# Block 2's projections as seven products of halves, with the weight sums made in place during block 0's FFN

## The chip, the cores and the metric

The kernel runs on one core of one Trainium2 chip. The metric is the device time of one launch in microseconds (us); smaller is better. A time comes from runs without a profile; the profile comes from one more execution, whose own time is given beside its span.

## What is computed

`x` is 4 sequences of 1024 tokens with 512 features in float32, 4096 tokens in all. The reference, cut to what matters:

```python
xn  = layernorm(x)
q, v, g = xn @ Wq.T, xn @ Wv.T, silu(xn @ Wg.T)        # three 512 x 512 projections
ret = scan(lam * state + v)                            # along the tokens of a sequence
out = (layernorm(q * ret) * gamma + beta) * g
x1  = x + layernorm(out @ Wo.T)
h   = layernorm(x1)
up, gate = (h @ fp8(up_w)) * us, silu((h @ fp8(gate_w)) * gs)      # 512 -> 1536
y   = x1 + layernorm(((gate * up) @ fp8(down_w)) * ds)             # 1536 -> 512
```

The FFN weights are rounded to fp8 values first, and the kernel also looks for weights that are too large for fp8 (the "search"), whose finding it adds to the output's scale.

## The kernel before

**Blocks and their overlap.** The tokens are cut into `NB` = 8 blocks of 512. A block has an attention part (class `Retention`) and an FFN part (class `Ffn`). The main loop (`for t in range(NB)`, line 973) does three things at once: the FFN of block t (`f`), the attention of block t+1 (`b`), and the loading, normalizing and transposing of block t+2 (`n`); `l` is the FFN of block t-1, of which the last layernorm and the store are left. Each turn of `t` has twelve steps `i`, one for each 128 of the 1536 hidden features. I write "turn t" and "step i" for these.

**Order.** Every engine's instructions run in the order in which the program writes them (`InOrder`, lines 66 to 74), so the order within a step is the schedule of all five engines. All profile lines therefore name line 74, and one tells instructions apart by their tiles. SyncE issues nearly all transfers (DMAs), in program order too; a transfer that must wait for data holds back those behind it.

**A step.** TensorE does the gate product (tile `pfg`), some attention work, the up product (`pfu`), and the down product (`pd`) of step i-2. Between them ScalarE does the silu of the gate, VectorE multiplies up and gate (`f.fuse`, line 1082: tile `gate<-pfu`), and ScalarE rounds that for the down product (`fuse<-gate`). `pfg` and `pfu` take turns in two PSUM banks (`ps_f`), so the up product of step i+1 can't begin before VectorE's multiplication of step i has read its bank.

**Two ways to project.** A block with `t < FAST` = 3 projects with the stored weights `wv_sb`, `wq_sb`, `wg_sb`: twelve groups of 128 output features, eight matmul instructions of 512 tokens each (functions `v`, `q`, `g_of`). A block with `t >= FAST` splits each weight matrix and its input into halves both ways and forms seven products of halves in place of eight (`product`, line 461; `order` lists them). Seven times three products need sums of input halves (`input_sums`, on GpSimd, tile `t_sums`) and sums of weight halves (`weight_sums`, tiles `sum_v` and so on). The weight sums are made once by VectorE in turn 1, steps 0 and 1, and kept in DRAM; from there they stream through `w_ring`, four slots of 256 KB, one fetch for each product, issued when a slot is free. `t_sums`, `w_ring` and `mids` lie in the places of `wv_sb`, `wq_sb` and `wg_sb`, and the first four fetches are issued at the end of turn 1, step 6.

**The end of an attention part.** In steps 7 to 10 the output projection of 128 tokens each is made (`b.o`, line 1067, tile `po`), and with it runs a chain across four engines for each group s of 128 tokens:

- `o_moments(s)` (step s+7): VectorE takes the statistics of `po`, GpSimd turns the variance into 1/std with two small instructions (`rstd_in_place`, line 262).
- `x1_of(s)` (same step, behind `f.fuse`): ScalarE normalizes `po` in blocks 0 and 1 (`shift_scale`, three instructions; VectorE does it in later blocks), GpSimd adds it to `x`, SyncE keeps the sum in DRAM (`kept`).
- `x1_moments(s)` (head of step s+8): VectorE takes the statistics of that sum, GpSimd makes 1/std.
- `x1n_of(s)`, `move_x1n(s)` (step s+8, ahead of `o_moments(s+1)` and `f.fuse`): ScalarE normalizes the sum, VectorE transposes it by 32 x 32 blocks, SyncE sends it through DRAM (`mxs`) to finish the transposition. The last group (s = 3) is transposed by TensorE instead (`turn_x1n(3)`, tile `pt`, step 11).

VectorE's statistics of `x`, its transposition, its statistics of the next `po` and its `f.fuse` stand in one queue in this order.

**The search.** 24 ScalarE instructions (tile `seen`) in turn 1, dealt out over the steps by the list `look`; `pass_over` brings their finding to `ds_sb` in turn 2, step 1.

Of the kernel before, what the change touches and what calls it, by code (L numbers as in the profile page):

```python
# [10 lines left out]
F32 = mybir.dt.float32  # L11
I32 = mybir.dt.int32
F32R = mybir.dt.float32r
F8 = mybir.dt.float8e4
AF = mybir.ActivationFunctionType
ALU = mybir.AluOpType

P = 128
# [5 lines left out]
def retention_ffn_sandwich(  # L24
# [20 lines left out]
    NT, D = x.shape  # L45
# [182 lines left out]
    def find_over():  # L228


        k = 0
        for j in range(4):
            for w in (gate_sb, up_sb, down_sb):
                v = w[:, ts(j, NI // 4), :] if w is down_sb else w[:, :, ts(j, I // 4)]
                for sign in (1.0, -1.0):
                    tag = "ret" if k >= 6 else "xn"
                    seen = work.tile(list(v.shape), F8, tag=tag, name=f"seen_{k}", bufs=2 if k >= 6 else 1)
                    act.activation(
                        seen, v.bitcast(F32), AF.Relu, bias=neg_max, scale=sign,
                        accum_out=over[:, k : k + 1], saturate=False,  # L240
                    )
                    k += 1
                    yield
# [3 lines left out]
    def pass_over():  # L247

        dve.reduce_sum(total, over, mybir.AxisListType.X)
        po = ps_tile("over_all")  # L250
        pe.matmul(po[:, :1], mean_w, total, start=True, stop=True)
        dve.tensor_scalar(total, po[:, :1], 3e38, 3e38, ALU.mult, ALU.mult)
        dve.tensor_scalar(total, total, 0.0, None, ALU.mult)
        dve.tensor_scalar(ds_sb, ds_sb, total, None, ALU.add)

# [74 lines left out]
    FAST = 3  # L330
    H = TB // 2
# [4 lines left out]
    squares = {"v": (wvT, wv_sb), "q": (wqT, wq_sb), "g": (wgT, lambda: wg_sb)}  # L336
    operands = {}

    def weight_sums():

        for k, (src, w) in squares.items():
            w = w() if callable(w) else w
            v = src.rearrange("(c p) f -> p c f", p=P)
            a11, a12, a21, a22 = (w[:, i : i + 2, o : o + H] for o in (0, H) for i in (0, 2))
            operands[k] = {1: v[:, 0:2, 0:H], 2: v[:, 2:4, 0:H], 4: v[:, 2:4, H:D]}
            done = {}
            for j, x, y, op in (
                (5, a21, a22, ALU.add), (6, 5, a11, ALU.subtract),
                (7, a11, a21, ALU.subtract), (3, a12, 6, ALU.subtract),
            ):  # L350
                t = work.tile([P, D], F32, tag="tok", name=f"sum_{k}{j}", bufs=4)
                done[j] = t.rearrange("p (c f) -> p c f", c=2)
                x, y = (done[o] if isinstance(o, int) else o for o in (x, y))
                dve.tensor_tensor(done[j], x, y, op)
                operands[k][j] = dram.tile([P, 2, H], F32, tag=f"sum_{k}{j}", name=f"dsum_{k}{j}", bufs=1)
                sp.dma_start(operands[k][j], done[j])
                yield

    sums = weight_sums()
# [481 lines left out]
    wg_sb = load_square(wgT, "wg_sb")  # L841
    a = Retention(0, x_first)
# [128 lines left out]
    look = [2, 2, 2, 0, 1, 3, 3, 3, 2, 2, 2, 2]  # L971
    l = None
    for t in range(NB):
        f, n = Ffn(a), None
        fast = b is not None and b.fast
        for i in range(NI):
# [5 lines left out]

            if l and i == 0:
                l.fetch()
# [6 lines left out]
            if l and b and not fast and i == 3:  # L991
                l.norm(0)
                l.add(0)
                l.norm(1)
                l.add(1)
# [8 lines left out]
            if n and i == 6 and t > 0:  # L1004
                n.stats(2)
                n.stats(3)
                n.rstd()
                if n.fast:
                    n.shift()
# [11 lines left out]
            if fast and i in (0, 1, 2, 3, 4, 5, 6):  # L1021
                b.product()
            if fast and i == 2:
                l.stats(0)
# [9 lines left out]
            if b and not fast and t > 0 and i < 3:  # L1034
                b.v(i + 1)
                b.scan(i + 1)
            if l and b and not fast and i == 2:
                l.stats(0)
                l.stats(1)
            if b and not fast and i == 3:  # L1040
                b.halves()
                units()
                if t == 0:
                    rounds(3, now=False)
                b.g_of(0)
                b.mean()
                b.center_y()
                if t == 0:
                    n.stats(3)
                    n.rstd()  # L1050
                    n.shift()
            if b and not fast and i == 4:
                b.halves()
                if t == 0:
                    rounds(3, now=False)
                b.g_of(1)
                b.var()
# [3 lines left out]
            if b and not fast and i == 6:  # L1061
                b.g_of(3)
                b.z(2)
                if t == 0:
                    b.z(3)
# [12 lines left out]
            if n and n.fast and i == 11:  # L1078
                n.input_sums(1, 2)
# [3 lines left out]
            if b and not fast and i == 4:  # L1083
                b.rstd_y()
            if n and i == 11:
                if n.fast:
                    n.products(2)
                else:
                    n.v(0)
                    n.scan(0)  # L1090
                b.turn_x1n(3, "pf")
                b.upper_of(3)
            if fast and i < 6:
                b.product()
# [27 lines left out]
            if l and b and not fast and i == 2:  # L1122
                l.stats(2)
                l.stats(3)
                l.rstd()
# [5 lines left out]
            if l and b and not fast and i == 3:  # L1131
                l.norm(2)
                l.add(2)
                l.norm(3)
                l.add(3)
            if b and not fast and t > 0 and i < 3:
                b.q(i + 1)
                b.y_of(i + 1)
            if b and not fast and i == 6 and t > 0:
                b.z(3)  # L1140
            if n and i == 5 and t == 1:
                n.stats(0)
                n.stats(1)
# [6 lines left out]
            if n and t > 0 and 6 <= i <= 9:  # L1150
                n.norm_x(i - 6, n.fast)
                n.send_x(i - 6)
# [7 lines left out]
            if n and i == 11:  # L1160
                if n.fast:
                    n.product()
                    n.input_sums(3, 4)
                else:
                    n.q(0)
                    n.y_of(0)
# [24 lines left out]
            if n and n.fast and i == 11:  # L1191
                n.product()
            if n and t > 1 and i == 5:
                n.stats(0)
                n.stats(1)
            if t == 1 and i < 2:
                for _ in range(6):
                    next(sums, None)
            if t == 1 and i == 6:
# [7 lines left out]
            if t == 2 and i == 1:  # L1207
                pass_over()
# [73 lines left out]
```

## Time and profile before

| | |
|---|---|
| median of 3 runs | 992.09 us (991.88 to 992.85) |
| the profiled execution, its own time | 991.89 us |
| its span, first to last instruction | 990.1 us |
| TensorE busy | 968.6 us, 98% |
| VectorE, ScalarE, GpSimd busy | 66%, 37%, 26% |
| granted TensorE clock, mean | 0.998 |
| turn 0, from its first gate product to that of turn 1 | 106.05 us |
| turn 1 | 124.78 us |
| turn 2 | 119.99 us |
| turns 3, 4, 5 | 118.59, 118.61, 118.60 us |
| turn 6 | 112.30 us |

In a line of the timeline the first number is the start in us from the start of the span, the second the time in us (of all xN instructions together); then come the engine, the operation, the tile written and the tiles read, and in brackets how long the engine sat idle before it and for whom. The list of busy time by stretches gives start:end, length, and the busy time and number of instructions of each engine.

### The profile page before, as it was taken

What the parts mean: (1) busy time and instruction counts of PE and PEld (TensorE: products, weight loads), DVE (VectorE), ACT (ScalarE), POOL (GpSimd) and SP (SyncE); (2) the same over time, 40 slices, a digit from 0 to 9 for tenths busy, and PEclk for the clock granted to TensorE, in tenths of its full rate; (3) what the DMA queues carried; (4) which work ended last, traced back from release to release, by engine and by line L of the source; (5) the groups of instructions that cost most, each with busy time, mean ns of one, the idle gap of its engine ahead of it and who ended that gap; (6) DMA issues with size and microseconds to landing.
All of it is one profiled execution on the core that took longest, in us unless ns stands there. A gap on an engine that the chain in (4) does not pass through costs nothing.

```text
span 990.1 us, 11037 instructions
## 1 busy us (share of the span) xinstructions
PE 968.6 (98%) x3878; PEld 722.0 (73%) x3878; DVE 657.1 (66%) x1006; ACT 365.3 (37%) x549; POOL 256.4 (26%) x337
## 2 busy tenths in 40 slices
PE   9999999999999999999999999999999999999996
PEld 7455766666666878678876788767887788877885
DVE  5996978548746567665686566866567656756445
ACT  3556575433765125221432114321152211512223
POOL 1405121203314033240513305132141312322020
PEclk9999999999999999999999999999999999999999
DMA  9312314412136326253243633245241542213021
GB/s 295 119 64 73 119 64 104 130 64 85 65 98 149 126 69 229 80 144 118 85 128 90 160 91 109 94 129 157 76 149 57 136 138 75 75 32 117 0 86 43
DMA packets 85223, 104.56 MB, mean 106 GB/s; under 512 B 7728, under 2 KB 49712, under 8 KB 85168
## 3 DMA queue, kind: packets, MB, share of 16 engines
q1 hardware_dynamic: 83584, 102.92, 34.5%
q10 hardware_dynamic: 1584, 0.94, 0.5%
q8 instruction: 31, 0.51, 0.2%
q14 instruction: 24, 0.20, 0.1%
HBM read 71.06 MB, written 32.77 MB: 105 GB/s over the span
## 4 chain that ended last, share of the span: by engine, by line
PE 86%; DVE 6%; POOL 3%; ACT 2%; issue 1%; DMA 1%; ACTq 0%; DVEq 0%; SPq 0%; POOLq 0%
PE pfu L74 16%; PE pfg L74 16%; PE pd L74 15%; PE pv L74 10%; PE pg L74 10%; PE pq L74 9%; PE po L74 9%; POOL t_sums L74 1%; DVE st L74 1%; DVE fuse L74 1%; POOL mv L74 1%; DVE scr L74 1%; ACT seen L74 1%; POOL x L74 1%; DVE d L74 1%
## 5 line engine op out<-in xcount | busy, mean ns | idle before, releaser
L74 PE MATMUL pfu<-x1nT,up_sb 128*128 128x512 f32 x768 | 212.1, 418 | 0.0
L74 PE MATMUL pfg<-x1nT,gate_sb 128*128 128x512 f32 x768 | 194.3, 395 | 0.4 <-DVE x1nT L74 0.4
L74 PE MATMUL pd<-down_sb,fuse 128*128 128x512 f32 x720 | 187.2, 401 | 0.0
L74 PEld LDWEIGHTS pfu<-x1nT,up_sb 128*128 128x128 f32 x768 | 144.5, 188 | 44.4 <-issue 14.4
L74 PEld LDWEIGHTS pfg<-x1nT,gate_sb 128*128 128x128 f32 x768 | 144.1, 188 | 30.4 <-DVE x1nT L74 0.8
L74 PEld LDWEIGHTS pd<-down_sb,fuse 128*128 128x128 f32 x720 | 135.3, 188 | 29.3 <-issue 1.7
L74 ACT CAST fuse<-gate 128x512 fp32r<-128x512 f32 x90 | 55.7, 618 | 236.4 <-DVE gate L74 236.4
L74 ACT ACTIVATE gate<-pfg,gs_sb 128x512 f32<-128x512 f32 x96 | 65.7, 684 | 206.2 <-PE pfg L74 206.1
L74 DVE SCALAR_TENSOR_TENSOR gate<-pfu,us_sb,gate 128x512 f32<-128x512 f32 x96 | 71.6, 746 | 82.8 <-PE pfu L74 82.8
L74 PE MATMUL po<-wo_sb,y 128*128 128x512 f32 x256 | 114.5, 592 | 0.0
L74 POOL TENSOR_SCALAR mv<-mv 128x1 f32<-128x1 f32 (+1 forms) x82 | 18.6, 226 | 302.6 <-DVE mv L74 301.6
L74 PEld LDWEIGHTS po<-wo_sb,y 128*128 128x128 f32 x256 | 48.2, 189 | 50.3 <-issue 46.9
L74 DVE TENSOR_TENSOR fuse<-gate,fuse 128x512 fp32r<-128x512 f32 x90 | 75.6, 840 | 9.1 <-ACT fuse L74 9.1
L74 POOL TENSOR_TENSOR ysum<-y 128x256 f32<-128x256 f32 (+1 forms) x13 | 13.5, 1038 | 188.8 <-DVE y L74 161.1
L74 POOL TENSOR_TENSOR x<-x,x1n 128x512 f32<-128x512 f32 x32 | 46.7, 1460 | 45.7 <-DVE x1n L74 36.7
L74 DVE BATCH_NORM_STATS2 st<-x 128x6 f32<-128x512 f32 x64 | 43.6, 681 | 13.7 <-POOL x L74 11.2
L74 DVE TENSOR_TENSOR mids<-pv,mids 128x512 f32<-128x512 f32 x25 | 17.3, 691 | 46.3 <-PE pv L74 43.4
L74 POOL TENSOR_TENSOR mv<-mv,nhalf 128x1 f32<-128x1 f32 (+1 forms) x75 | 45.3, 604 | 6.2
L74 PE MATMUL pv<-xnT,wv_sb 128*128 128x512 f32 (+1 forms) x120 | 42.9, 508 | 1.6 <-ACT xnT L74 1.6
L74 PE MATMUL pv<-t_sums,w_ring 128*128 128x256 f32 x160 | 38.3, 382 | 5.6 <-POOL t_sums L74 5.6
L74 PE MATMUL pq<-xnT,wq_sb 128*128 128x512 f32 (+1 forms) x112 | 43.4, 531 | 0.0
L74 PE MATMUL pg<-xnT,wg_sb 128*128 128x512 f32 x96 | 43.0, 592 | 0.0
(156 smaller groups left out, 1334.5 us busy)
## 6 DMA issues: line engine op xcount, KB each, us to landing
kept<-x SPq DMA_DIRECT2D x32, 256.0 KB, 2.1
x<-kept SPq DMA_DIRECT2D x32, 256.0 KB, 3.7
x<-in_x SPq DMA_DIRECT2D x28, 256.0 KB, 4.1
out<-d SPq DMA_DIRECT2D x27, 256.0 KB, 2.0
xnT<-mx SPq DMA_DIRECT2D x24, 256.0 KB, 4.8
mxs<-xs SPq DMA_DIRECT2D x84, 64.0 KB, 1.8
x1n<-mxs SPq DMA_DIRECT2D x21, 256.0 KB, 2.7
mx<-xn SPq DMA_DIRECT2D x20, 256.0 KB, 2.3
```

The source lines that it names most:

```text
L74: return lambda *args, **kwargs: tc.keep_in_program_order(op(*args, **kwargs))
```

## The change

- `FAST` is 2: block 2 uses the seven products too. It begins them in turn 0, step 11, and goes on in turn 1, which gets the order of steps that turns 2 to 6 have. The weight sums are needed one turn earlier.
- `weight_sums` runs on GpSimd, four instructions for each of q, v and g, in place of the weights, at the end of steps 7, 8 and 9 of turn 0. `keep_sums` sends each set to DRAM one step later. The first four fetches into `w_ring` are issued at the end of turn 0, step 10.
- In step 11 all four `input_sums` stand together; of v's products, one comes ahead of the transposition `turn_x1n(3)`, one behind it and one at the end of the step (before: two, one and one). The fourth moves to step 1 of the next turn.
- The search is dealt out as 5, 5, 4, 2, 0, 0, 0, 2, 2, 2, 2, 0 over turn 1's steps, and its scratch tiles change their tags.
- `pass_over` becomes a generator whose three parts stand in turn 2, step 0, between products.
- Branches that only a slow block in turn 1 used are gone (among them VectorE's scans and normalizations there).

The diff, cut to its core:

```diff
     def pass_over():
         dve.reduce_sum(total, over, mybir.AxisListType.X)
-        po = ps_tile("over_all")
+        yield
+        po = ps_tile("over_all", "pa0")
         pe.matmul(po[:, :1], mean_w, total, start=True, stop=True)
+        yield
         dve.tensor_scalar(total, po[:, :1], 3e38, 3e38, ALU.mult, ALU.mult)
...
-    FAST = 3
+    FAST = 2
...
-    def weight_sums():
-        for k, (src, w) in squares.items():
...
-                dve.tensor_tensor(done[j], x, y, op)
-                operands[k][j] = dram.tile([P, 2, H], F32, tag=f"sum_{k}{j}", name=f"dsum_{k}{j}", bufs=1)
-                sp.dma_start(operands[k][j], done[j])
-                yield
+    def weight_sums(k):
...
+        pool.tensor_tensor(a22, a21, a22, ALU.add)
+        pool.tensor_tensor(a21, a11, a21, ALU.subtract)
+        pool.tensor_tensor(a11, a22, a11, ALU.subtract)
+        pool.tensor_tensor(a12, a12, a11, ALU.subtract)
+        return {5: a22, 7: a21, 6: a11, 3: a12}
+
+    def keep_sums(k, done):
+        for j, t in done.items():
+            operands[k][j] = dram.tile([P, 2, H], F32, tag=f"sum_{k}{j}", name=f"dsum_{k}{j}", bufs=1)
+            sp.dma_start(operands[k][j], t)
...
-    look = [2, 2, 2, 0, 1, 3, 3, 3, 2, 2, 2, 2]
+    look = [5, 5, 4, 2, 0, 0, 0, 2, 2, 2, 2, 0]
...
+            if t == 2 and i == 0:
+                next(passing)
...
-            if b and not fast and t > 0 and i < 3:
-                b.v(i + 1)
-                b.scan(i + 1)
...
-            if n and n.fast and i == 11:
-                n.input_sums(1, 2)
+            if n and i == 11:
+                n.input_sums(1, 2, 3, 4)
             units()
             f.up(i)
             f.fuse(i)
...
             if n and i == 11:
-                if n.fast:
-                    n.products(2)
-                else:
-                    n.v(0)
-                    n.scan(0)
+                n.product()
                 b.turn_x1n(3, "pf")
                 b.upper_of(3)
+                n.product()
...
             if fast and i < 6:
-                b.product()
+                b.products(2 if i == 1 else 1)
...
-            if n and i == 11:
-                if n.fast:
-                    n.product()
-                    n.input_sums(3, 4)
-                else:
-                    n.q(0)
-                    n.y_of(0)
+            if t == 0 and 8 <= i < 11:
+                keep_sums("qvg"[i - 8], done)
             if i == f.lag:
                 f.sums()
             if f.lag <= i < (NI if b else NI - 1):
                 f.down(i - f.lag)
...
-            if n and n.fast and i == 11:
+            if n and i == 11:
                 n.product()
+            if t == 0 and 7 <= i < 10:
+                done = weight_sums("qvg"[i - 7])
...
-            if t == 1 and i < 2:
-                for _ in range(6):
-                    next(sums, None)
-            if t == 1 and i == 6:
+            if t == 0 and i == 10:
                 t_sums = wpool.tile([P, 4, 2, H], F32, tag="wv_sb", name="t_sums")
                 w_ring = wpool.tile([P, RING, 2, H], F32, tag="wq_sb", name="w_ring")
                 mids = wpool.tile([P, 4, 2, H], F32, tag="wg_sb", name="mids")
                 for _ in range(RING):
                     fetch_weights()
...
-            if t == 2 and i == 1:
-                pass_over()
```

## The prediction

> **What bounds the kernel now.** I read the page first, then TensorE's timeline cut at the first gate product of each turn, then the timeline of all engines late in turn 0.
>
> ```profile
> PE 968.6 (98%) x3878; PEld 722.0 (73%) x3878; DVE 657.1 (66%) x1006; ACT 365.3 (37%) x549; POOL 256.4 (26%) x337
> ...
> 95.21:201.26 106.05, 104.03 (x378) 70.34 (x377) 80.98 (x111) 59.91 (x89) 20.84 (x30) 1.00 0.37 105
> 201.26:326.04 124.78, 122.32 (x442) 82.23 (x440) 81.71 (x121) 67.05 (x94) 35.59 (x40) 1.00 0.32 95
> 446.03:564.62 118.59, 117.48 (x499) 92.86 (x497) 78.56 (x123) 33.95 (x52) 34.25 (x45) 1.00 0.40 114
> ```
>
> TensorE is busy all the time (turns 0, 1 and 3 are shown), so its work is the time, and anything that makes it wait adds. What a way of projecting costs is read from starts:
>
> ```profile
> 145.87 3.59 PE L74 MATMUL pg<-xnT,wg_sb 128*128 128x512 f32 x8
> 148.90 2.39 PE L74 MATMUL pfu<-x1nT,up_sb 128*128 128x512 f32 x8
> 151.12 1.98 PE L74 MATMUL pd<-down_sb,fuse 128*128 128x512 f32 x8
> ...
> 563.08 1.89 PE L74 MATMUL pv<-t_sums,w_ring 128*128 128x256 f32 x8
> 564.62 2.20 PE L74 MATMUL pfg<-x1nT,gate_sb 128*128 128x512 f32 x8
> 566.65 1.89 PE L74 MATMUL pv<-t_sums,w_ring 128*128 128x256 f32 x8
> ```
>
> An ordinary group takes 3.03 us to the next start, and the FFN product behind it 2.22 instead of 1.81: 3.44 together. A product of halves takes 1.54 + (2.03 - 1.81) = 1.76.
>
> But 98% hides how tight turn 0's end is. One turn of the four-engine chain there:
>
> ```profile
> 173.12 1.27 POOL L74 TENSOR_TENSOR x<-x,x1n 128x512 f32<-128x512 f32 x1 [1.76 <-ACT x1n L74]
> 174.42 0.69 DVE L74 BATCH_NORM_STATS2 st<-x 128x6 f32<-128x512 f32 x1 [1.95 <-POOL x L74]
> 175.42 0.19 POOL L74 TENSOR_SCALAR mv<-mv 128x1 f32<-128x1 f32 x1 [1.03 <-DVE mv L74]
> 176.28 0.29 ACT L74 ACTIVATE nb<-nb,mv 128x1 f32<-128x1 f32 x1 [0.66 <-POOL mv L74]
> 176.61 0.82 ACT L74 ACTIVATE x1n<-x,nb,mv 128x512 f32<-128x512 f32 x1
> 177.46 0.71 DVE L74 STREAM_TRANSPOSE xs<-x1n 128x512 f32<-128x512 f32 x1 [2.13 <-ACT x1n L74]
> 178.10 0.66 DVE L74 BATCH_NORM_STATS2 st<-po 128x6 f32<-128x512 f32 x1
> 178.89 0.72 DVE L74 SCALAR_TENSOR_TENSOR gate<-pfu,us_sb,gate 128x512 f32<-128x512 f32 x1
> ```
>
> Each line starts when the one above ends. The last, f.fuse, starts the round again over ScalarE's normalization of `po` to the next add (181.64): 8.5 us a round, against TensorE's 8.88 a step. GpSimd's 74% of idle time lies inside this chain, so it is not free.
>
> **What the Trainium skill says.** "GPSIMD Engine Reference", section 3.1, puts a two-input elementwise operation there at about 2.6 cycles an element. The trace agrees that it is slow: 512 elements take 1.26 to 1.32 us on GpSimd (`t_sums` below), and the like took 0.68 on VectorE. "SBUF — State Buffer", section "Who interferes with whom", says that VectorE with two SBUF inputs and GpSimd exclude each other. The trace agrees: VectorE's rest product at 164.24 took 1.75 us beside a GpSimd add (1.48 itself) and 0.69 at 171.78 without one. "TensorE: Matmul & The Clock Gate", Part 1, says that an idle window of about 3.4 us halves the clock until a busy one has passed. No run here shows it: the longest wait in the turns is 1.37 us and the clock is 1.00 in each.
>
> **The change, part by part.** Sums are against the profiled execution, 991.89 us (span 990.1 and 1.8 around it); the median of the runs is 0.2 above.
>
> *Products.* Turn 0, step 11: two groups (6.88) become three products (5.28): -1.6. Turn 1, steps 0 to 6, lasted 73.46 (201.26 to 274.72); turn 3's lasted 69.01 (446.03 to 515.04), and the fourth product in step 1 adds 1.76: -2.7. In later turns that product only moves from step 11 to the next turn's step 1: 0.
>
> *v's order.*
>
> ```profile
> 554.52 1.26 POOL L74 TENSOR_TENSOR t_sums<-xnT 128x512 f32<-128x512 f32 x1
> 555.86 1.32 POOL L74 TENSOR_TENSOR t_sums<-xnT,t_sums 128x512 f32<-128x512 f32 x1
> 557.14 1.27 POOL L74 TENSOR_TENSOR t_sums<-xnT 128x512 f32<-128x512 f32 x1
> 558.38 1.26 POOL L74 TENSOR_TENSOR t_sums<-xnT,t_sums 128x512 f32<-128x512 f32 x1
> ```
>
> v's second product waits 1.1 us for the second of these in each of turns 1 to 5. The sums don't move; the transposition (0.44 from start to start) moves into the wait, and its input is ready at 556.06, when the first product ends. So 0.44 goes and 0.67 stays: 5 x 0.44 = -2.2. The 1.34 us for which turn 1's first product waits, with xnT's transfers just in, stays, as the same searches precede them in steps 8 and 9.
>
> *pass_over.* Its product waited 0.96 for VectorE's reduction. A whole product will stand between: -1.0.
>
> *Search.* Up to five instructions of 1.57 + 0.19 us in a step, 8.8, on top of 1.3 to 1.9 that ScalarE does in steps 0 to 2 of turn 3; the steps last 10.7 to 12.5. They fit, with two to spare ahead of the fuse cast at most. Without that cover each would cost TensorE up to 1.76. VectorE loses the weight sums and the slow scans. I take 0; bounds 0 and +2.
>
> *Weight sums in turn 0.* Four dependent GpSimd instructions in each of steps 7 to 9. No row shows them; by form and chaining the four `t_sums` above are nearest, 5.1 us from 554.52 to 559.64. They stand on GpSimd behind the add of group s and ahead of 1/std of the same group. Queued behind them is `mv<-mv`, for which ScalarE's `x1n` waits, for that VectorE's transposition, and behind that f.fuse. Today 1.03 us pass from the add's end (174.39) to `mv` (175.42), in the first round 1.46. So rounds grow by 5.2 - 1.5 = 3.75, then 4.2 and 4.2. TensorE may lead f.fuse by one step only:
> - step 8's f.fuse ends 171.09 + 3.75 = 174.84; step 9's `pfu` starts at 175.56: hidden.
> - step 9's ends 179.61 + 7.95 = 187.56; step 10's `pfu` wants 184.45: a wait of 3.1.
> - step 10's ends 188.12 + 12.15 = 200.27; step 11's `pfu`, 5.85 after the one before, wants 193.45: a wait of 6.8.
>
> It ends at 202.1 instead of 192.1. Bounds for the four: 5.05 (4 x 1.26) and 5.9 (4 x 1.48, the add beside VectorE): -0.4 to +2.5 over three rounds. A gain is excluded, since TensorE leaves this stretch no idle time to win.
>
> *Fetches.* The first `w_ring` fetches stand on SyncE behind `kept` of the last group and g's four sums.
>
> ```profile
> 191.47 0.34 SPq L74 DMA_DIRECT2D kept<-x  x1
> ...
> w_ring<-in_wvT SPq DMA_DIRECT2D x15, 256.0 KB, 3.2
> ```
>
> `kept` moves to 191.47 + 12.15 = 203.6. Five issues at some 0.45 us make 205.8. Landing: 3.2 median alone, but 1 MB of stores runs ahead, so I take 3.7 (that of `x<-kept`, four in a row); bounds 2.5 and 6.2, the shortest and longest of `w_ring`. v's first product starts at 209.5, and behind it come 1.76, 0.44, 1.76, 1.81 and 1.76: turn 1 begins at 217.0 instead of 201.26, +15.8. That holds the -1.6 already. After 7.4 idle us the clock should be halved for a window of 3.4 us: an estimate by the skill's page of +1.7, bounds 0 and 3.4.
>
> *Other transfers.* The 12 stores of sums go from turn 1 to turn 0 behind adds that are done; each issue is about 0.35 us of SyncE: 0.
>
> Sum: 15.8 + 1.7 - 2.7 - 2.2 - 1.0 = **+11.6**: 1003.5 for the profiled execution, 1003.7 against the median. Own range 1000.5 to 1010.5 from the bounds above.
>
> **Rivals.**
> - *The chain waits, the ring doesn't* (the weights land earlier than I think). The transposition then waits for `x1n` of the last group (ready at 194.47 + 12.15 = 206.6), the second product for `t_sums` (208.1), and turn 1 begins at 213.5: +12.2 - 5.9 = +6.3, 998.4. For: the ring's tile is free early. Against: the fetches stand behind `kept` in the program. Chance 0.08.
> - *The sums find cover; only the ring waits.* `kept` stays at 191.47, weights land about 197.4, wanted at 192.1: +5.3 - 1.6 - 5.9 = -2.2, with a slow clock -0.5: 989.9 to 991.6. Chance 0.10.
> - *Faster: everything finds cover.* -1.6 - 5.9 = -7.5, 984.6. For: GpSimd is 74% idle. The place is the gap between add and 1/std. TensorE's slack is 4.5 us in step 8 (171.09 to 175.56) and 0.4 more a round, so three sets hide if a round grows by under 1.8, four sums in under 2.8, or 0.7 each. The trace's 1.26 stands against it. Chance 0.06.
> - *Worse than my sum*: the search or a second cold clock as well, over 1010. Chance 0.04.
>
> That block 2 is not really made cheaper can be excluded: the same products run in blocks 3 to 7.
>
> **How the numbers follow.** My case has 0.72. Its time is the prediction. The range must leave out 0.2 at most: 995 to 1010 holds about 0.70 of mine and the 0.08 of the first rival. Faster by over 0.2% (2 us; about what a measurement of this kernel can tell from no change): 0.06, and 0.04 of the second rival, 0.10. Same: 0.06. Slower: 0.72 + 0.08 + 0.04 = 0.84.
>
> **What would show it.** Right: in turn 0, steps 8 to 10, four GpSimd instructions of 1.3 us between `x<-x,x1n` and `mv<-mv`; waits of about 3 and 7 us before `pfu`, released by VectorE's `gate`; one of about 7 before v's first product, released by a transfer; turn 0 some 122 to 124 long, turn 1 119.5 to 120.5, turns 2 to 5 about 118.2. Wrong: sums of 0.7 us or less, or 1/std ahead of them, or turn 0 under 110.

## The result and the profile after

| | before | after |
|---|---|---|
| median of 4 runs | 992.47 us (991.88 to 992.85) | 1005.44 us (1004.54 to 1006.38) |
| the profiled execution, its span | 991.89, 990.1 | 1006.38, 1004.6 |
| mean granted TensorE clock | 0.998 | 0.985 |
| turn 0 | 106.05 | 126.81 |
| turn 1 | 124.78 | 119.30 |
| turn 2 | 119.99 | 118.39 |
| turns 3, 4, 5 | 118.59, 118.61, 118.60 | 118.13, 118.14, 118.18 |
| turn 6 | 112.30 | 114.00 |

The change makes the kernel slower: the ratio is 1.0131 (95% interval 1.0114 to 1.0149), 13.0 us. In the profiled executions turn 0 is 20.8 longer, turns 1 to 6 together are 6.7 shorter, and 0.5 lies before and behind them: +14.5.

The page's line of TensorE, and the busy time in turns 0, 1 and 3 (start:end, length, then the busy time and number of instructions of TensorE, its weight loads, VectorE, ScalarE and GpSimd, then the clock):

```profile
PE 972.4 (97%) x3950; PEld 740.0 (74%) x3950; DVE 651.9 (65%) x1007; ACT 369.6 (37%) x556; POOL 276.0 (27%) x358
```

```profile
95.42:222.23 126.81, 110.37 (x386) 76.61 (x385) 79.65 (x109) 60.31 (x90) 41.45 (x46) 0.91 0.40 116
222.23:341.53 119.30, 118.11 (x499) 92.82 (x497) 76.30 (x122) 71.49 (x100) 34.14 (x45) 1.00 0.39 113
459.92:578.05 118.13, 117.64 (x498) 92.88 (x497) 78.44 (x123) 33.76 (x52) 34.27 (x45) 1.00 0.39 114
```

TensorE is still busy 97% of the span, and for 3.8 us more than before although it has less to multiply. Two things are hidden in that share: 16.4 us without work in turn 0 (126.81 - 110.37), and a mean clock of 0.91 there, which makes the same work count as more busy time. Turn 1, now with products of halves, is only 1.2 longer than turn 3.

One round of the chain, in the timeline of all engines, to hold against the round shown of before:

```profile
178.37 1.29 POOL L74 TENSOR_TENSOR x<-x,x1n 128x512 f32<-128x512 f32 x1 [1.75 <-ACT x1n L74]
179.62 5.36 POOL L74 TENSOR_TENSOR wv_sb<-wv_sb 128x512 f32<-128x512 f32 x4
...
185.07 0.19 POOL L74 TENSOR_SCALAR mv<-mv 128x1 f32<-128x1 f32 x1
...
185.93 0.29 ACT L74 ACTIVATE nb<-nb,mv 128x1 f32<-128x1 f32 x1 [5.02 <-POOL mv L74]
...
187.10 0.71 DVE L74 STREAM_TRANSPOSE xs<-x1n 128x512 f32<-128x512 f32 x1 [6.49 <-ACT x1n L74]
...
188.53 0.72 DVE L74 SCALAR_TENSOR_TENSOR gate<-pfu,us_sb,gate 128x512 f32<-128x512 f32 x1
```

The statistics of the group are ready at 180.61 (0.69 from 179.70, then 0.18), but `mv` starts at 185.07, behind the four weight sums. ScalarE idles 5.02 us for it and VectorE 6.49. The adds start at 164.84, 178.37, 191.28 and 204.17: 13.5, 12.9 and 12.9 us apart, where before they were 9.2, 8.5 and 8.5 apart (163.96, 173.12, 181.64, 190.15). TensorE's timeline shows the three places where this arrives:

```profile
189.30 3.02 PE L74 MATMUL pfu<-x1nT,up_sb 128*128 128x512 f32 x8 [2.53 <-DVE gate L74]
...
202.19 3.78 PE L74 MATMUL pfu<-x1nT,up_sb 128*128 128x512 f32 x8 [5.54 <-DVE gate L74]
...
212.34 3.75 PE L74 MATMUL pv<-xnT,w_ring 128*128 128x256 f32 x8 [6.37 <-DMA w_ring<-in_wvT]
```

The last wait is for the weights, and SyncE's lines in the timeline say why they come late:

```profile
205.47 0.34 SPq L74 DMA_DIRECT2D kept<-x  x1
...
205.86 2.56 SPq L74 DMA_DIRECT2D dsum_g<-wg_sb  x4
...
208.46 0.61 SPq L74 DMA_DIRECT2D w_ring<-in_wvT  x1
```

The last `kept` waits for the late add. The fetch stands behind it and behind four stores of sums whose data had long been ready. A fourth cost shows in the busy time of the same stretch, cut into pieces of 5 us (the clock is the number behind GpSimd's):

```profile
205.00:210.00 5.00, 0.97 (x3) 0.25 (x1) 1.52 (x3) 2.34 (x5) 3.81 (x6) 0.50 0.92 303
210.00:215.00 5.00, 2.66 (x6) 2.16 (x7) 0.00 (x0) 0.00 (x0) 2.29 (x2) 0.50 0.75 221
215.00:220.00 5.00, 5.00 (x20) 4.16 (x19) 0.87 (x2) 1.17 (x2) 0.00 (x0) 0.75 0.17 52
```

The product at 212.34 took 3.75 us for eight instructions that take 1.96 at full clock (experiment 11). In the Trainium skill, "TensorE: Matmul & The Clock Gate", Part 1, says that an idle window of about 3.4 us halves the clock. The trace of the kernel before could not show it; here the clock is 0.50 behind waits of 5.54 and 6.37 us. The length of 3.4 is not confirmed: behind the wait of 2.53 the clock was 0.66 over the next 5 us.

### The profile page after: what moved, and what is told of

The parts are those of the page before. It is cut to its first block, busy times and chain, and to the rows that moved or that the text cites. A ratio compares the mean times of both kernels' runs of the same rounds, so it can differ in the third digit from the quotient of the medians.

```text
span 1004.6 us, 11260 instructions
## 1 busy us (share of the span) xinstructions
PE 972.4 (97%) x3950; PEld 740.0 (74%) x3950; DVE 651.9 (65%) x1007; ACT 369.6 (37%) x556; POOL 276.0 (27%) x358
## 4 chain that ended last, share of the span: by engine, by line
PE 78%; DVE 9%; POOL 5%; ACT 4%; issue 2%; DMA 1%; SPq 0%; ACTq 0%; DVEq 0%; POOLq 0%
PE pfu L74 14%; PE pfg L74 14%; PE pd L74 14%; PE pv L74 10%; PE pq L74 9%; PE pg L74 8%; PE po L74 8%; DVE st L74 1%; DVE fuse L74 1%; POOL t_sums L74 1%; POOL mv L74 1%; DVE scr L74 1%; POOL x L74 1%; ACT x1n L74 1%; DVE xs L74 1%
## 5 line engine op out<-in xcount | busy, mean ns | idle before, releaser
L74 PE MATMUL pfu<-x1nT,up_sb 128*128 128x512 f32 x768 | 214.9, 423 | 8.1 <-DVE gate L74 8.1
L74 PEld LDWEIGHTS pfu<-x1nT,up_sb 128*128 128x128 f32 x768 | 146.4, 191 | 51.7 <-issue 12.9
L74 DVE TENSOR_TENSOR mids<-pv,mids 128x512 f32<-128x512 f32 x30 | 20.7, 692 | 53.2 <-PE pv L74 47.7
L74 DVE BATCH_NORM_STATS2 st<-x 128x6 f32<-128x512 f32 x64 | 43.6, 681 | 13.9 <-POOL x L74 11.2
L74 PE MATMUL pv<-t_sums,w_ring 128*128 128x256 f32 x192 | 46.2, 384 | 2.0 <-POOL t_sums L74 2.0
L74 PE MATMUL pg<-t_sums,w_ring 128*128 128x256 f32 x192 | 45.7, 381 | 0.6 <-ACT mids L74 0.6
L74 PE MATMUL pq<-t_sums,w_ring 128*128 128x256 f32 x192 | 45.3, 379 | 0.0
L74 PEld LDWEIGHTS pv<-t_sums,w_ring 128*128 128x128 f32 x192 | 36.2, 191 | 8.5 <-POOL t_sums L74 3.2
```

The costliest lines, as they stand in the source:

```text
L74: return lambda *args, **kwargs: tc.keep_in_program_order(op(*args, **kwargs))
```

## The experiments

Theory: the cost is one chain, weight sums ahead of 1/std on GpSimd, then f.fuse, then the last `kept`, then the fetch on SyncE, then a slow clock; the products, v's order and `pass_over` bring some 6 us. Rivals: that the chain's own end (`x1n`, `t_sums`) holds the turn whether the fetch is early or late; that the sums cost by the work that they add on GpSimd or by contention, wherever they stand. "The port" in the expectations is the one that VectorE and GpSimd share in the Trainium skill, "SBUF — State Buffer", section "Who interferes with whom"; the traces show slowed instructions, not a port. Each ratio is to the kernel before in the same series. Edits are to the changed kernel unless said otherwise.

**1. The fetch one step earlier.** Only the ring's tile and the fetches move; `t_sums` and `mids` stay.

```diff
+            if t == 0 and i == 9:
+                w_ring = wpool.tile([P, RING, 2, H], F32, tag="wq_sb", name="w_ring")
+                for _ in range(RING):
+                    fetch_weights()
             if t == 0 and i == 10:
-                w_ring = wpool.tile([P, RING, 2, H], F32, tag="wq_sb", name="w_ring")
...
-                for _ in range(RING):
-                    fetch_weights()
```

> Only the first four weight fetches and the ring's tile move, from the end of step 10 to the end of step 9 of turn 0, so that they stand ahead of the last kept transfer and of g's stores. Theory (chain of 1/std behind the GpSimd sums, and then the ring): the two waits before the up products of steps 10 and 11 stay at 2.5 and 5.5 us; v's first product follows the up product of step 11 (end 205.9 in the changed kernel's profile) at once instead of at 212.3. Turn 1 begins at about 215 to 216 instead of 222.2, and the time falls by 6 to 7 us to some 998 to 999.5. Rival (the chain alone holds everything and the ring's wait only stands in front of other waits: the transposition's input, t_sums): at most 2 us fall, to 1003 to 1004. Rival (more DMA traffic is the cause): no change, 1005.

Measured: 998.86 us, ratio 1.0064 (1.0044 to 1.0083). The waits for `gate` are the same, 2.54 and 5.53; the wait for the ring is gone, 0.75 for `t_sums` is left, and turn 1 starts at 214.71 instead of 222.23. So the late fetch is worth 5.9 us of the 13.0 (13.0 less 7.1; 6.6 between the two medians as they stand), and the rival that the chain's end would take its place falls.

**2. The sums behind 1/std**, with edit 1 as well.

```diff
                 b.x1_moments(i - 8)
+            if t == 0 and 8 <= i < 11:
+                done = weight_sums("qvg"[i - 8])
...
-            if t == 0 and 7 <= i < 10:
-                done = weight_sums("qvg"[i - 7])
```

> As the early fetch, and the twelve GpSimd instructions stand in steps 8 to 10 behind 1/std of the kept sum instead of ahead of it; same instructions, same steps but one later. Theory (the place in GpSimd's queue decides): each set now delays only 1/std of the output projection by about 2.5 us, of which ScalarE's cast hides 0.6, so a round grows by about 2 instead of 4.2; step 11's up product waits about 2, the transposition of the last group about 5, and turn 1 begins near 207 to 209: 992 to 994.5, close to the kernel before. Rival (GpSimd's use of the SBUF port it shares with VectorE slows VectorE, wherever the sums stand in these steps): like the early fetch alone, 998 to 1000.

Measured: 995.78 us, ratio 1.0042 (1.0026 to 1.0058), above what I expected and below the rival's 998 to 1000. Putting the sums behind 1/std doesn't take them out of the loop: they then stand ahead of the `po` statistics' 1/std of the next group, and the next add starts 11.2 us after the one before (190.59, 201.83). In the profiled execution a wait of 2.67 stayed before step 11's `pfu` and one of 5.20 before the transposition of the last group, which the clock then followed down (0.58 over 205 to 210). That execution, at 999.48, was the slowest of six, so its waits are no measure of the median. A GpSimd block of 5.35 us has no place in a round whose free stretches are shorter than that (2.8, 1.8 and 1.0 us in the kernel before).

**3. The sums in steps 4 to 6**, ahead of the chain, stores and fetches earlier too.

```diff
-            if t == 0 and 8 <= i < 11:
-                keep_sums("qvg"[i - 8], done)
+            if t == 0 and 5 <= i < 8:
+                keep_sums("vqg"[i - 5], done)
...
-            if t == 0 and 7 <= i < 10:
-                done = weight_sums("qvg"[i - 7])
+            if t == 0 and 4 <= i < 7:
+                done = weight_sums("vqg"[i - 4])
...
-            if t == 0 and i == 10:
+            if t == 0 and i == 8:
```

> The sums of v, q and g stand at the end of steps 4, 5 and 6 of turn 0, ahead of the chain, their stores one step later, the first fetches at the end of step 8. Theory (nothing but the chain and the ring costs time): turn 0 gets 1.6 us shorter than before, there is no wait before up products or v's first product, and the whole gain of 7.5 us (less 0.65 that the search costs in turn 1) is seen: 984.5 to 986.5. VectorE rounds weights in these steps and is 84% busy, so sharing the port may take up to 3 us of that. Rival (port or traffic): VectorE falls behind in steps 4 to 7, up products wait for it there, and the time is 990 or more.

Measured: 997.75 us, ratio 1.0051 (1.0034 to 1.0068). My theory, as I had put it, fell here: outside the chain the sums still cost nearly as much as inside it with the early fetch (6.0 against the 7.1 of experiment 1). Its timeline of all engines:

```profile
130.40 7.92 POOL L74 TENSOR_TENSOR wv_sb<-wv_sb 128x512 f32<-128x512 f32 x4
...
132.63 2.32 DVE L74 TENSOR_TENSOR scr<-scr 128x1024 f32<-128x1024 f32 x1
...
134.99 2.20 DVE L74 TENSOR_TENSOR up_sb<-scr 128x1024 fp32r<-128x1024 f32 x1
...
146.76 1.28 ACT L74 ACT_TABLE_LOAD   x1 [8.26 <-DVE fuse L74]
...
148.79 3.78 PE L74 MATMUL pfg<-x1nT,gate_sb 128*128 128x512 f32 x8 [4.71 <-ACT gate L74]
```

The same two VectorE products in the kernel before:

```profile
131.64 1.22 DVE L74 TENSOR_TENSOR scr<-scr 128x1024 f32<-128x1024 f32 x1
...
132.89 1.22 DVE L74 TENSOR_TENSOR up_sb<-scr 128x1024 fp32r<-128x1024 f32 x1
```

Beside the sums they take 2.32 and 2.20, and the set itself 7.92 (the next ones 6.72 and 6.37) instead of 5.4. Steps 4 to 6 are where VectorE rounds FFN weights; pushed back there, it made ScalarE wait 8.26 us (6.02 before) and TensorE 4.71 in step 6. Another 2.73 us of wait came in step 11, before the transposition; its cause was not taken apart. The skill's section has the rule that the two exclude each other, and I had used it in the prediction for one add; what I missed is its size when both have a long queue. The price of the sums depends on the neighbours, not only on the place in the chain.

**4. v's order alone**, on the kernel before.

```diff
-                n.input_sums(1, 2)
+                n.input_sums(1, 2, 3, 4)
...
-                    n.products(2)
+                    n.product()
...
                 b.turn_x1n(3, "pf")
                 b.upper_of(3)
+                if n.fast:
+                    n.product()
             if fast and i < 6:
-                b.product()
+                b.products(2 if i == 1 else 1)
...
-                if n.fast:
-                    n.product()
-                    n.input_sums(3, 4)
-                else:
+                if not n.fast:
```

> The kernel before with v's new order alone (all four input sums together, one product ahead of the transposition, the fourth moved to step 1 of the next turn); FAST stays 3. Theory: the transposition moves into the wait for t_sums, 0.44 us in each of five turns, 2.2 us in all: 990.2, the wait 0.4 to 0.7 instead of 1.1. Rival (the input sums 3 and 4 ahead of other work, or the ring with four products in one step, take it back): 992 or more.

Measured: 989.38 us, ratio 0.9976 (0.9969 to 0.9984), 2.4 below before: this part is a gain by itself, and the wait for `t_sums` is 0.40 a turn instead of 1.13.

**5 and 6. No weight sums**, with the fetch late (as in the changed kernel) and early (as in 1).

```diff
-        pool.tensor_tensor(a22, a21, a22, ALU.add)
-        pool.tensor_tensor(a21, a11, a21, ALU.subtract)
-        pool.tensor_tensor(a11, a22, a11, ALU.subtract)
-        pool.tensor_tensor(a12, a12, a11, ALU.subtract)
```

> The changed kernel without its twelve GpSimd additions (the weight sums are left out: what is stored and multiplied in their place is the unsummed halves); stores and fetches stand where they stand in it. It measures the ring's wait without the chain's. Theory: no wait before the up products of steps 10 and 11; the last kept transfer is issued at about 191.5, g's stores take 3 us of SyncE, the first weights land 4 us later, near 198.4, and v's first product, wanted at 192.1, waits 6 us, after which the clock is halved for a while. Turn 1 begins at 206 to 208.5. With the 6.7 us that turns 1 to 6 gained in the changed kernel's profile: 990.5 to 993.5. Rival (sums are what delays the ring; without them weights are in time): 985.

> As the one before (weight sums left out), with the first fetches at the end of step 9. Theory: neither wait is left; what remains in step 11 is the transposition's wait for its input and the wait for t_sums, together some 1.5 us. Turn 1 begins near 201, the time is 984.5 to 986, which is what the products, v's order and the split search are worth with the sums for nothing. Rival (further costs of the change that neither the chain nor the ring explains, traffic or the search): over 988.

Measured: 994.22 us, ratio 1.0014 (1.0006 to 1.0022), and 990.94 us, ratio 0.9986 (0.9978 to 0.9993). With the changed kernel and experiment 1 that gives four corners, each as the difference to before in its own series:

| | fetch at the end of step 10 | of step 9 |
|---|---|---|
| with the sums | +13.0 | +7.1 |
| without | +2.0 | -1.2 |

The sums are worth 8.3 to 11 us and the late fetch 3.3 to 5.9; each corner is known to 1 to 2 us, so the two ends of these ranges are hardly apart. With the fetch late and no sums the ring's wait alone is left, and the slow clock with it, in TensorE's timeline:

```profile
201.33 3.75 PE L74 MATMUL pv<-xnT,w_ring 128*128 128x256 f32 x8 [7.51 <-DMA w_ring<-dsum_v]
...
211.27 1.04 PE L74 MATMUL pfg<-x1nT,gate_sb 128*128 128x512 f32 x3
```

It is 9.94 us from that product to turn 1, as in the changed kernel. But the last corner missed: I had expected about 985. Its timeline of all engines shows a third wait, which in the changed kernel was hidden behind the ring's:

```profile
196.31 2.81 SPq L74 DMA_DIRECT2D dsum_g<-wg_sb  x4
...
202.21 0.59 ACT L74 COPY mids<-pv 128x512 f32<-128x512 f32 x1 [2.67 <-DMA w_ring<-in_wvT]
...
202.85 0.91 PE L74 MATMUL pv<-xnT,w_ring 128*128 128x256 f32 x3 [2.86 <-ACT mids L74]
```

`mids` lies in the place of `wg_sb`. Its first copy can't start before g's four stores have read that, and these stand on SyncE behind the last `kept` and x1n's transfers. v's third product waits 2.86 us for it. (The bracket names a fetch as what ScalarE waited for. It is the transfer that came last by the records; the stores are my reading, and experiments 8 and 9 test it.) The wait is 2.9 of the some 6 us missed. The median lies 1.5 above this execution, and most of the other runs had a lower mean clock (0.991 to 0.996 against 0.998); the rest was not taken apart.

**7. The sums in small pieces**: one or two at a time, in the gaps of each round, one of them on VectorE; order v, q, g; the ring in v's place, filled at the end of step 9; the search moved out of step 3.

```diff
-        pool.tensor_tensor(a22, a21, a22, ALU.add)
...
+        pending.extend(sums)
...
+            if t == 0 and 8 <= i < 11:
+                add_some(2)
             f.gate(i)
...
                 b.o_moments(i - 7)
+            if t == 0 and 7 <= i < 11:
+                add_some(2 if i == 7 else 1)
...
+            if t == 0 and i == 8:
+                add_some(1, dve)
...
-    look = [5, 5, 4, 2, 0, 0, 0, 2, 2, 2, 2, 0]
+    look = [5, 5, 6, 0, 0, 0, 0, 2, 2, 2, 2, 0]
```

> All sums are made. They stand in GpSimd's gaps: two in step 7 behind 1/std of the output projection; in steps 8 to 10 two behind 1/std of the kept sum and one behind that of the projection; one on VectorE in step 8 while it waits for the add. The ring takes the place of v's weights and is filled at the end of step 9. The search has 5, 5, 6, 0 in its first steps. Theory (only the place in the queue costs): two additions of 1.3 us fit the 2.8 us between the two 1/std of a step and one the 1.7 us ahead of the add, so that a round grows by 0.5 us at most and the chain ends 0.5 to 1.5 us later than without sums: 984.5 to 987. Rival (twelve additions of 1.3 us on GpSimd cost by their length or by the shared port): 990 or more.

Measured: 991.26 us, ratio 0.9986 (0.9979 to 0.9992). The time missed what I expected and lies where the rival put it, over 990. But experiment 6, which makes no sums at all, stands at 990.94: by the medians the sums in pieces cost 0.3 us, or about 1 with the gain in turn 1 below, so that most of what is missing is not theirs. The rounds came out as expected, 9.0 us. The first add came late, at 166.59 instead of 164.18 in experiment 6: the two sums ahead of it, in step 7, took 4.24 us beside VectorE's work, where pairs in later steps took 2.67. TensorE's waits are now 1.00 for `gate`, 1.10 for the ring, 1.65 before the transposition, 0.73 for `t_sums` and 2.44 for `mids`: five small ones where three large ones stood. Turn 1 is 118.51, 0.8 shorter, with no wait for the search.

**8. The down product ahead of the transposition** in step 11, on 7.

```diff
                 n.product()
+                f.down(i - f.lag)
                 b.turn_x1n(3, "pf")
                 b.upper_of(3)
-                n.product()
...
             if n and i == 11:
-                n.product()
+                n.products(2)
```

> As the spread sums, and in step 11 the down products stand right behind v's first product, then the transposition, then v's second and third products. Theory: the down products (1.81 us) cover the waits for the transposition's input and for t_sums; the 0.4 us of t_sums goes in five turns and up to 1.5 us in turn 0: 2 to 3.5 us below the spread sums, 981 to 984. Rival (VectorE's rest products then come too late for the next gate product): no gain over the spread sums.

Measured: 986.86 us, ratio 0.9937 (0.9922 to 0.9951). Turns 2 to 5 lose their wait for `t_sums` (0.40) and last 117.2 to 117.5, 0.9 less. The wait for `mids` grows to 3.77, so the time stays above what I expected. In the timeline of all engines the stores are now the releaser by name:

```profile
201.39 0.62 ACT L74 CAST x1nT<-x1n 128x512 fp32r<-128x512 f32 x1 [2.72 <-DMA x1n<-mxs]
...
205.27 0.59 ACT L74 COPY mids<-pv 128x512 f32<-128x512 f32 x1 [2.74 <-DMA dsum_g<-wg_sb]
```

**9. The stores of q's and g's sums from ScalarE's queue**, on 8.

```diff
-                keep_sums(k, done[k])
+                keep_sums(k, done[k], sp if i == 8 else act)
```

> As the spread sums with the down products first, and q's and g's stores are issued from ScalarE's queue instead of SyncE's. In the run before, v's third product waited 3.8 us for ScalarE's copy, which waited for g's stores (their place becomes the copy's target), and these stood on SyncE behind the last kept transfer. Theory (SyncE's order is the third place where the change waits): q's and g's stores leave 4 to 6 us earlier, the first weights arrive 2.8 us earlier, the waits of 0.6 and 3.8 go: 981 to 984. Rival (the copy waits for the last transposed group's transfer ahead of it on ScalarE): no more than 1 us, 986.

Measured: 983.26 us, ratio 0.9904 (0.9887 to 0.9920), as expected. The wait for `mids` falls from 3.77 to 1.52 and turn 0 from 112.81 to 109.65. Nothing but the queue of eight stores was changed, so 2.25 us of the third wait were theirs: the order on SyncE. The 1.52 that are left are the rival of the expectation. ScalarE's copy now follows its own work without a gap (202.45), but ahead of it a cast waits for the transfer of the third group's transposition, in the timeline of all engines:

```profile
190.06 5.14 SPq L74 DMA_DIRECT2D mxs<-xs  x4
...
201.41 0.62 ACT L74 CAST x1nT<-x1n 128x512 fp32r<-128x512 f32 x1 [3.28 <-DMA x1n<-mxs]
```

**10. Two fetches at the end of step 9 and two at the end of step 10**, on 9.

```diff
             if t == 0 and i == 9:
...
-                for _ in range(RING):
-                    fetch_weights()
+                fetch_weights()
+                fetch_weights()
             if t == 0 and i == 10:
...
+                fetch_weights()
+                fetch_weights()
```

> As the one with the stores on ScalarE's queue, with only two of the four first fetches at the end of step 9 and the other two at the end of step 10, so that SyncE comes to the third group's transposition 1.2 us sooner. Theory: the rounded copy of that group on ScalarE, and the copy behind it, come 1 us sooner: 0 to 1 us below the one with four. Rival: the third product's weights then come too late and it is slower.

Measured: 981.93 us, ratio 0.9889 (0.9874 to 0.9903): 1.1% below the kernel before, and the lowest of all here, though its interval overlaps that of 9. The step that was meant is in the trace: SyncE issues the four transfers of the third group's transposition in 1.80 us instead of 5.14, ScalarE's cast comes at 197.94 instead of 201.41, the wait for `mids` is gone, and turn 0 falls from 109.65 to 107.85. Why the issues had taken 5.14 stays open. Among TensorE's waits, the three that are left of this case (the first is 1.16 in turn 0):

```profile
PE pt L74 <- ACT x1n L74: 1.4, 2, 1.2
...
PE pfu L74 <- DVE gate L74: 1.0, 1, 1.0
PE pv L74 <- POOL t_sums L74: 0.7, 1, 0.7
```

So the same products and the same sums, in other places, make the kernel faster than before. Turn 0 is 1.8 above before, and the rest of the launch gives back some 12. Not all of that is the change's own: v's order gave 2.4 on the kernel before, and the place of the down product, worth 0.9 in each of turns 2 to 5, was not tried there.

**11. The array kept busy during the wait**: the changed kernel with 20 products that nobody uses.

```diff
             if n and i == 11:
+                if t == 0:
+                    warm_bank = ps_tile("warm_bank", "pa1")
+                    for _ in range(20):
+                        pe.matmul(warm_bank[:, :P], mean_w, mean_w, start=True, stop=True)
                 n.product()
```

> The changed kernel with 20 products of 128 columns, whose result nobody uses, ahead of v's first product in turn 0's step 11, where TensorE waits 6.4 us for the ring. They put nothing ahead of the wait's end [...]. Theory (the clock is halved because TensorE idled): the clock is full again at 212, v's first products, the transposition and the down products take 7.5 us to turn 1 instead of 9.9, and the time falls by 2 to 2.5 us to 1003. Rival (the products behind the wait are slow for another reason, such as late weights or t_sums): no change, 1005.4.

Measured: 1004.17 us, ratio 1.0129 (1.0112 to 1.0146). TensorE's timeline, and the stretches to hold against those of the changed kernel:

```profile
211.94 1.96 PE L74 MATMUL pv<-xnT,w_ring 128*128 128x256 f32 x8 [1.78 <-DMA w_ring<-dsum_v]
...
219.26 1.04 PE L74 MATMUL pfg<-x1nT,gate_sb 128*128 128x512 f32 x3
```

```profile
205.00:210.00 5.00, 5.00 (x41) 4.97 (x39) 1.20 (x3) 2.34 (x5) 4.16 (x5) 0.88 0.92 294
210.00:215.00 5.00, 3.22 (x18) 2.76 (x17) 0.00 (x0) 1.06 (x2) 1.52 (x2) 1.00 0.56 188
```

The weights land at the same time (211.94 against 212.34), but from there to turn 1 it is 7.32 us instead of 9.89: 2.6 us of the change's cost are the clock alone. The whole time doesn't show it: against the kernel before of its own series the cost is 12.6 us instead of 13.0, where I had expected 2 to 2.5 less, and the intervals overlap. The stretch is what shows it.

## Why the prediction came out as it did

Predicted +11.6 us and 1003.7; the medians give +13.0 and 1005.44, the profiled executions +14.5. The mechanism was the one on record: three waits at the places named, each with the releaser named. Turn 0 was too small by 3.5 and the rest gained 0.6 more than I said, so the total, 2.9 off against the profiled execution, is a little closer than its parts. By its own steps, with turn 1's start as the measure of turn 0:

| step of the sum | predicted | measured |
|---|---|---|
| first add of the chain | as before, 163.96 | 164.84 |
| four sums on GpSimd | 5.1 (5.2 in the rounds) each set | 5.78, 5.36, 5.35 |
| three rounds, more than before | 12.15 | 13.14 |
| delay of `pfu`, start against start wanted, steps 10 and 11 | 3.1, 6.8 | 3.09, 5.71 (idle 2.53, 5.54) |
| last `kept` | 203.6 | 205.47 |
| SyncE, from there to the first fetch | 2.2 | 2.99 |
| landing | 3.7 | 3.88 |
| v's first product | 209.5, waits 7.4 | 212.34, idle 6.37 |
| from there to turn 1, clock included | 7.5 + 1.7 | 9.89 |
| turn 1 starts | 218.7 | 222.23 |
| everything behind that | -5.9 | -6.5 |

**Turn 0, too small by 3.5.** Four terms were under-sized, all on the same side. *The sums*: an instruction takes 1.28 us, as in the `t_sums` row that I took, but each needs the one before, so 1.36 pass from start to start, and one of the first set took 1.71 beside a VectorE product. A set took 0.3 to 0.7 more than I said, within my bounds: 1.0 over the rounds. *SyncE*: the four stores took 2.56, some 0.64 each, and not 0.45: 0.8, with 0.2 for the landing. *The clock*: 2.35 over the 7.54 of full speed, and not 1.7: 0.7. That the clock would be halved at all was read from the skill's page; that it cost this stretch its time is shown by experiment 11. *The start*: 0.9, most likely because step 4 ran at a lower clock in this execution (below); the forecast could not have it, nor does every execution have it (experiment 11's step 4 ran at full clock). The two delays of `pfu` came as the mechanism says. I had counted from the start that `pfu` wanted, and the profile's idle time begins only when the modelled end of the product before is past; counted alike, step 10's is 3.09. Step 11's is 1.1 shorter than predicted because the first wait had lowered TensorE's clock too (0.66 over 190 to 195): `pfu` and `pd` took 3.02 and 2.71, and it came later itself.

**The search, taken at 0, cost more.** In turn 1's step 4 TensorE waits 0.65 for `mids`, and the step lasts 12.1 instead of 11.2: a `seen` of 1.56 us in step 3 stands ahead of ScalarE's squares and copies. Experiment 7, which puts nothing in step 3, has 11.2 and no such wait. It lay inside my bound of 2.

**v's order was worth what I said.** Turns 3 to 5 are 0.42 to 0.47 shorter, 0.44 on record, and experiment 4, on the kernel before, gives 2.4 in all against 2.2. The wait for `t_sums` alone fell by more, to 0.40 of 1.13 and not 0.67; some 0.3 came back elsewhere in the turn.

**A wait that I said would stay is gone.** Turn 1's first product waited 1.34 us for xnT; it doesn't now. I argued that the same searches precede the transfers in steps 8 and 9. In the changed kernel the transfers are issued 3.65 us ahead of step 11's gate product, before 2.36 ahead. Steps 5 to 7 lost seven searches (3, 3 and 3 to 0, 0 and 2), which would explain it; that was not taken apart. Together the search (0.9 more) and this (1.3 less) put turn 1 at 119.30, just under the 119.5 to 120.5 on record, and make most of the difference between -5.9 and -6.5.

**What was not on the list.** I priced "everything finds cover" at 984.6 as if the chain and the ring were all that could wait. Experiment 6 took both away and stopped at 990.94, on `mids`, which waits for stores on SyncE. I had costed those stores at 0, as transfers of data that is ready; they are also what frees a tile. In the changed kernel this was hidden, so it changed no number of the forecast, but the rival's price was wrong by it.

**Two readings.** "GpSimd's 74% of idle time lies inside this chain" says too much: 74% is of the whole span, and the chain holds only the idle time of steps 7 to 10. The round shown there leaves out short instructions without a mark (VectorE's aggregation, GpSimd's second one of 0.55 us), and only with them does each line start when the one above ends.

**The rivals.** "Chain only" (998.4) is what experiment 1 sets up: 998.86. "Only the ring waits" (989.9 to 991.6) is experiment 5: 994.22, some 3 above; the ring's wait there is 7.5 and not 5.3. "Everything covered" took more than covering the sums and the fetch (experiments 8 to 10), and ended lower than its price, at 981.93, helped by the down product ahead of the transposition, which removes what is left of the `t_sums` wait in turns 1 to 5. The price asked for sums of 0.7 us or less; none was that short, and cover came from their places.

## What to carry to other kernels

GpSimd was idle for 74% of the span, but where the sums were put its idle time lay inside a chain: before placing work there, find the free stretches between the instructions of the chain, and cut the work into pieces that fit them (5.35 us ahead of a 0.2 us instruction cost 8 to 11 us; the same work in pieces of one or two left waits of 1.0 and 1.65 us). Outside the chain, look at what the engine beside it is doing. Look next at the queue that the late result releases: a transfer that waits for data holds back every fetch behind it, and a store of ready data can hold the tile that somebody else needs. When the first wait of a place is taken away, expect a second and a third behind it, and let an experiment without the suspected work tell how far down the next one lies.

## What the runs showed of the hardware

A wait costs TensorE twice. After the long waits of the changed kernel (5.54, then 6.37) the clock was 0.50, and it was full again only some 5 us after work had resumed (0.50 in 210 to 215, 0.75 in 215 to 220); the price was 2.35 to 2.6 us on 7.5. Around a wait of 2.5 us it went both ways: 0.66 over the 5 us after 2.53 idle us in the changed kernel, and after 2.44 in experiment 7 (a product of 1.89 us took 3.49), but 1.00 after 2.86 in experiment 6 (1.99). So the length of the wait alone doesn't decide.

Short waits can do it too. In turn 0's step 4 TensorE waits 1.36 and 0.22 us for `half`, in every kernel here. In some executions the clock stays full, in others it falls, as in the profiled one of the changed kernel (over 130 to 135: 0.72), and the step lasts 13.1 us instead of 11.5. The changed kernel's four runs lie in two pairs, 1004.54 and 1004.60, 1006.29 and 1006.38, and the profiled one is the highest; that would fit, but for the runs without a profile it isn't shown. What decides it stays open.

VectorE and GpSimd with two SBUF inputs each slowed one another, VectorE by a factor of 1.9 and GpSimd of 1.5, when both had a long queue of such work (2.32 against 1.22, 7.92 against 5.36): both at once, and GpSimd by more than the one add in the prediction (1.48 against 1.27).
